# Where GpSimd stops making pauses between indirect DMAs: from the first blocks of the second L1 mixture on

## The chip, the cores and the metric

The kernel runs on one core of a Trainium2 chip. Its time is the device time of one execution, in microseconds (us). A core has these engines: TensorE (PE, with its weight loads shown as PEld), VectorE (DVE), ScalarE (ACT), GpSimd (POOL) and SyncE (SP). Each works through its own queue of instructions in order; semaphores tie them together. Sixteen DMA engines move data between the memories.

## The reference

The input is x, 2048 tokens of 256 features, float32. Two layers follow one another, each made of half a mixture of experts, attention, and half a mixture of experts again:

```python
x = x + 0.5 * moe_L0(layernorm(x))
x = x + attn_L0(layernorm(x))      # a recurrent key-value mix and a channel mix
x = x + 0.5 * moe_L0(layernorm(x))
x = x + 0.5 * moe_L1(layernorm(x))
x = x + attn_L1(layernorm(x))      # linear attention with rotary embedding
x = x + 0.5 * moe_L1(layernorm(x))
```

A mixture scores each token for every expert, takes the best K of them, and adds the weighted outputs of those experts, each of the form `(silu(x @ wg) * (x @ wu)) @ wd`, to that of a shared expert which sees every token. L0 has 8 experts of width 176 and K = 2, L1 has 32 experts of width 96 and K = 6; the shared widths are 352 and 192.

## The kernel before

**Tiles and halves.** The 2048 tokens are 16 tiles of 128. The L1 mixtures and the L1 attention are done in two halves of 8 tiles, A and B, and each half in two groups of 4 tiles. The names of tiles carry the half and the pass: `L_0A` and `L_0B` are the first L1 mixture, `L_1A` and `L_1B` the second, the one that the change is about.

**One mixture of a half** (`sparse_moe`, L402 on) has these steps.
- Routing and plan: scores, the best six, and for each pair of token and expert a slot in a table `xs` in device memory, sorted by expert in blocks of 128 slots. The last step for a group is its index tile (VectorE L576, `idx`).
- `scatter` (L584): GpSimd writes the normalized rows to their slots, by one indirect DMA (L590) for each tile and each of the six choices, so 24 calls a group and 48 a half (`xs_B<-axl_at` is the second mixture's half B).
- Blocks (`step`, L915): for each block of 128 slots SP loads it (`fetch`, L776, after all scatters of the half), PE transposes it (L785, copied by ScalarE at L789), PE multiplies with the expert's gate and up weights (`inner`, L807), ScalarE and VectorE make the gated product (`gates`, L688 and L689), PE turns it (L716, ScalarE L723), PE multiplies with the down weights (`outward`, L825), VectorE evicts the result as `yb` (L833) and SP stores it to `ys` (L835). Five blocks are in work at once, each a step behind the other. 66 blocks are always done; a `tc.If` (L980) holds the rest, for inputs that need more. With these inputs the rest is skipped.
- `gather` (L840): GpSimd fetches the outputs for a tile and a choice back, by an indirect DMA (L847) into one of eight `yk` buffers, again 24 calls a group. The first group's indices (`soon`) need only the first 36 blocks, the second group's (`idx`) need all.
- `add_back` (L858): VectorE adds the weighted rows to x (L859). The buffer is then free for another gather. When a token tile is complete, SP stores it to `out` (L683).
- Shared experts: PE L699, L716, L743 and VectorE L750 add to x. For half B of the second mixture they are spread over the end of its blocks and the time behind them.

**The order of the work** is partly planned while the program is built. `Clock` (L308) holds a planned time, lets a block take 1.41 us of it, a GpSimd call 1.27 (`CALL`) and a pause 1.14 (`PAUSE`), and decides from that between which blocks a call, an addition or a step of the plan is put. `combine` (L890) makes a gather when the planned GpSimd is free, and puts an addition in once more than four gathers are open. `in_turn` (L380) keeps GpSimd's calls in the order planned, `behind_blocks` (L390) puts VectorE's and PE's other work behind the blocks issued so far.

**The pauses.** `called` (L316) counts the GpSimd calls. After each third call `pause` (L326) issues five memsets of a tile `still`, 128 x 96 float32, on GpSimd, one after the other (L331 once, L334 four times); their result is used by nothing. The planner adds 1.14 us for them. A flag decides whether a pause is made:

```python
if len(self.row) == 3:
    if pauses["on"]:
        self.pause()
    else:
        self.row.clear()
        self.still = d.ins
```

The flag is off while the first L0 mixture and the second one send out their tokens (`begin`, L1400), on from there to the last block of the second L1 mixture's half B, and off behind it. Beside the blocks of 1A the 48 scatter calls of 1B are made, then the first group's gathers of 1A; beside those of 1B the second group's gathers of 1A and the first group's of 1B. The second group's gathers of 1B are the tail, after all blocks.

Of the kernel before, what the change touches and what calls it, by code (L numbers as in the profile page):

```python
# [57 lines left out]
def macaron_kernel(ctx: ExitStack, tc: tile.TileContext, a: dict, out: bass.AP):  # L58
# [247 lines left out]
    pauses = {"on": True}  # L306
# [1074 lines left out]
    def all_of(part):  # L1381
        for us in part:
            clock.run(us)
# [6 lines left out]
    def given_rows(m, groups, added, rank=0):  # L1390

        for g in groups:
            yield from wait(lambda: g in m["ready"])
            yield clock.now + 3.0
            yield from m["combine"](g, rank)
            if g == 0 and m["early"] is not None:
                yield from wait(lambda: 0 in m["whole"])
            added.add(g)
# [20 lines left out]
    def settle(*done):  # L1419

        while not all(d() for d in done):
            if fill:
                all_of(fill.pop(0))
            else:
                clock.run(1.0)
# [5 lines left out]
    def pieces_of(part):  # L1431

        return dict(step=lambda: next(part, None), fetch_ahead=lambda: None)

    def filled():
        while fill:
            all_of(fill.pop(0))
# [178 lines left out]
    shared_of(m2[0])  # L1616
    settle(lambda: 1 in sent2[0])
    filled()
    done = [set(), set()]
    clock.begin(4, given_rows(m2[0], range(2), done[0], 4))  # L1620
    all_of(m2[0]["blocks"](lambda: m2[1] if 1 in sent2[1] else None))
# [2 lines left out]
    clock.begin(5, given_rows(m2[1], range(2), done[1], 5))  # L1624
    part = m2[1]["shared"](0, HT)
    all_of(m2[1]["blocks"](lambda: pieces_of(part)))
    pauses["on"] = False
    all_of(part)
    settle(lambda: 1 in done[0], lambda: 1 in done[1])

# [52 lines left out]
```

## Time and profile before

| | |
|---|---|
| median of 6 runs | 1393.07 us (1382.71 to 1395.7) |
| profiled execution, its own time | 1393.51 us |
| its span | 1391.6 us |
| mean granted TensorE clock | 0.916 |
| busy: PE, PEld | 1250.1 us (90%), 950.1 us (68%) |
| busy: DVE, ACT, POOL | 705.5 us (51%), 601.2 us (43%), 653.1 us (47%) |
| scatter calls of 1B, first and last start | 1123.0, 1198.7 us |
| results of 1A's blocks 1, 36 and 66 evicted | 1117.9, 1193.5, 1236.9 us |
| results of 1B's blocks 1 and 66 evicted | 1238.5, 1346.2 us |
| gathers of 1A, first and last start | 1200.0, 1298.0 us |
| gathers of 1B, first and last start | 1303.1, 1382.5 us |

The page of a profile describes one execution. Its times count from the start of the span. A group of instructions is given by line, engine, operation, the tile written and the tiles read, the count, the busy time with the mean of one in ns, and behind a second bar the idle time of the engine just before them with what ended it. A view of waits lists an engine and its instruction, what ended the wait, and then the total, the number of times and the longest. In a table of windows each row is a stretch of the span, with its length and then the busy time and number of instructions of PE, PEld, DVE, ACT and POOL, the granted clock, the mean busy share of the DMA engines and GB/s. In a timeline each row has start and duration in us, and in brackets the idle time before and its releaser. The releaser "remote" stands where none of the core's instructions ends at the time at which the wait does; "issue" stands for time in which nothing that the profile shows was waited for.

### The profile page before, as it was taken

What the parts mean: (1) busy time and instruction counts of PE and PEld (TensorE: products, weight loads), DVE (VectorE), ACT (ScalarE), POOL (GpSimd) and SP (SyncE); (2) the same over time, 40 slices, a digit from 0 to 9 for tenths busy, and PEclk for the clock granted to TensorE, in tenths of its full rate; (3) what the DMA queues carried; (4) which work ended last, traced back from release to release, by engine and by line L of the source; (5) the groups of instructions that cost most, each with busy time, mean ns of one, the idle gap of its engine ahead of it and who ended that gap; (6) DMA issues with size and microseconds to landing.
All of it is one profiled execution on the core that took longest, in us unless ns stands there. A gap on an engine that the chain in (4) does not pass through costs nothing. (4 is left out here: it accounts for less than half of the span.)

```text
span 1391.6 us, 22823 instructions
## 1 busy us (share of the span) xinstructions
PE 1250.1 (90%) x6036; PEld 950.1 (68%) x6036; DVE 705.5 (51%) x2500; ACT 601.2 (43%) x1645; POOL 653.1 (47%) x1267
## 2 busy tenths in 40 slices
PE   7979999899998989999789988989897889989991
PEld 5757776466676757667568865967764677878861
DVE  5422366843424423565354556575576456455653
ACT  4313385775434323444234534544333344444430
POOL 1520344211102510577777557162767457656655
PEclk9879999999998889999969998998899789999995
DMA  9812432992008323433847764643322237778853
GB/s 285 253 65 79 136 117 69 302 324 77 0 0 187 112 87 111 131 114 102 235 142 244 240 206 135 200 132 103 129 85 80 91 124 224 242 216 249 258 155 100
DMA packets 193669, 213.64 MB, mean 154 GB/s; under 512 B 40669, under 2 KB 176509, under 8 KB 193533
## 3 DMA queue, kind: packets, MB, share of 16 engines
q1 hardware_dynamic: 168956, 144.91, 33.9%
q0 software_dynamic: 24576, 67.14, 15.8%
q8 instruction: 59, 0.97, 0.3%
q14 instruction: 78, 0.63, 0.2%
HBM read 101.99 MB, written 109.97 MB: 152 GB/s over the span
## 5 line engine op out<-in xcount | busy, mean ns | idle before, releaser
L847 POOL DMA_INDIRECT yk_L<-ys_L,idx_L x64 | 63.2, 987 | 189.3 <-DMA ys_L<-yb_L 142.8
L334 POOL MEMSET still<- 128x96 f32 x564 | 100.9, 179 | 32.3
L699 PE MATMUL pg_L<-L0sgu,xTs_L 128*128 128x352 f32 x256 | 106.4, 549 | 9.2 <-DVE h_L L689 5.6
L807 PE MATMUL pg_L_b<-L0gu,xbT_L 128*128 x312 | 108.6, 471 | 1.0 <-ACT xbT_L L789 0.6
L590 POOL DMA_INDIRECT xs_L<-xn_L,idx_L x64 | 61.7, 963 | 88.6 <-DVE taken_L L202 29.3
L825 PE MATMUL py_L_b<-L0down,hT_L_b 88*128 x312 | 81.4, 383 | 0.1
L699 PEld LDWEIGHTS pg_L<-L0sgu,xTs_L 128*128 128x128 f32 x256 | 53.1, 224 | 34.5 <-issue 13.7
L689 DVE TENSOR_TENSOR h_L_b<-g_L_b,pg_L_b 128x176 f32<-128x176 f32 x78 | 26.1, 335 | 93.6 <-ACT g_L_b L688 77.4
L825 PEld LDWEIGHTS py_L_b<-L0down,hT_L_b 88*128 88x128 f32 x312 | 59.1, 192 | 19.8 <-issue 1.0
L807 PEld LDWEIGHTS pg_L_b<-L0gu,xbT_L 128*128 128x128 f32 x312 | 55.0, 195 | 20.4 <-issue 1.6
L590 POOL DMA_INDIRECT xs_B<-axl_at,idx_L_1B x48 | 46.3, 965 | 36.9 <-DVE soon_L_1B L578 24.8
L590 POOL DMA_INDIRECT xs_A<-axl_at,idx_L_1A x48 | 46.4, 966 | 35.6 <-DVE soon_L_1A L578 23.6
L807 PE MATMUL pg_L_0B_b<-L1gu,xbT_L_0B 128*128 x264 | 59.1, 350 | 1.4 <-DVEq L980 1.3
L1075 PE MATMUL pkk_cm<-mk_cm,w_WkeyT 128*128 128x512 f32 x128 | 58.7, 594 | 1.4 <-ACT sk_cm L1176 0.9
L807 PE MATMUL pg_L_0A_b<-L1gu,xbT_L_0A 128*128 x264 | 58.8, 348 | 1.1 <-issue 0.8
L807 PE MATMUL pg_L_1B_b<-L1gu,xbT_L_1B 128*128 x264 | 55.7, 335 | 3.9 <-DVE x L859 3.6
L743 PE MATMUL py_L<-L0sdown,hT_L 128*128 128x256 f32 (+1 forms) x192 | 54.3, 421 | 5.1 <-issue 5.0
L1087 PE MATMUL pkv_cm<-w_WvalT,sk_cm 128*128 128x256 f32 x256 | 58.6, 379 | 0.1
L1087 PEld LDWEIGHTS pkv_cm<-w_WvalT,sk_cm 128*128 128x128 f32 x256 | 48.3, 190 | 13.7 <-issue 7.2
L807 PE MATMUL pg_L_1A_b<-L1gu,xbT_L_1A 128*128 x264 | 55.9, 334 | 1.1 <-ACT xbT_L_1A L789 0.4
L688 ACT ACTIVATE g_L<-pg_L 128x176 f32<-128x176 f32 x64 | 19.4, 317 | 84.7 <-PE pg_L L699 45.7
L590 POOL DMA_INDIRECT xs_A<-xn_L_0A,idx_L_0A x48 | 46.5, 969 | 16.1 <-issue 13.1
(667 smaller groups left out, 3296.9 us busy)
## 6 DMA issues: line engine op xcount, KB each, us to landing
xs_A<-zero SPq DMA_DIRECT2D x1, 10112.0 KB
xs_B<-zero SPq DMA_DIRECT2D x1, 10112.0 KB
xb_L<-xs_L SPq DMA_DIRECT2D x78, 128.0 KB
ys_L<-yb_L SPq DMA_DIRECT2D x78, 128.0 KB
xb_L_0A<-xs_A SPq DMA_DIRECT2D x66, 128.0 KB
ys_A<-yb_L_0A SPq DMA_DIRECT2D x66, 128.0 KB
xb_L_0B<-xs_B SPq DMA_DIRECT2D x66, 128.0 KB
ys_B<-yb_L_0B SPq DMA_DIRECT2D x66, 128.0 KB
```

The costliest lines, as they stand in the source:

```text
L334: d = nc.gpsimd.memset(still, 0.0)
L590: d = nc.gpsimd.indirect_dma_start(out=xs, out_offset=bass.IndirectOffsetOnAxis(ap=idx[:, t, k : k + 1], axis=0), in_=sent[g][t - BT * g], ...
L688: nc.scalar.activation(g, pg[:, 0:width], AF.Silu)
L689: nc.vector.tensor_tensor(dst, g, pg[:, width : 2 * width], ALU.mult)
L699: nc.tensor.matmul(pg, xbT[:, c, i * P : (i + 1) * P], w["sgu"][:, c, u, :, :].rearrange("p z w -> p (z w)"), start=(c == 0), stop=(c == D ...
L743: nc.tensor.matmul(py, hT[0:m, k, :], w["sdown"][0:m, k, :], start=(k == 0), stop=(k == len(rows) - 1),)
L807: nc.tensor.matmul(pg, xbT[:, c, :], w["gu"][:, c, bass.ds(e, 1), :, :].rearrange("p e z h -> p (e z h)"), start=(c == 0), stop=(c == DC - 1),
L825: mm = nc.tensor.matmul(py, hT[0:HP, k, :], w["down"][:, bass.ds(e, 1), k, :].rearrange("p e d -> p (e d)"), start=(k == 0), stop=(k == C ...
L847: d = nc.gpsimd.indirect_dma_start(out=yk, out_offset=None, in_=ys[0 : (n + lead) * P, :], in_offset=bass.IndirectOffsetOnAxis(ap=of[:, t, ...
L1075: nc.tensor.matmul(ps, w[:, c, oc * P : (oc + 1) * P], src[:, c, :], start=(c == 0), stop=(c == DC - 1),)
L1087: nc.tensor.matmul(ps, src[:, c, i * P : (i + 1) * P], w[:, c, :], start=(c == 0), stop=(c == n - 1),)
```

## The change

One line moves: the flag goes off before the blocks of 1A, not behind those of 1B. No other line differs.

```diff
     settle(lambda: 1 in sent2[0])
     filled()
+    pauses["on"] = False
     done = [set(), set()]
     clock.begin(4, given_rows(m2[0], range(2), done[0], 4))
     all_of(m2[0]["blocks"](lambda: m2[1] if 1 in sent2[1] else None))
...
     clock.begin(5, given_rows(m2[1], range(2), done[1], 5))
     part = m2[1]["shared"](0, HT)
     all_of(m2[1]["blocks"](lambda: pieces_of(part)))
-    pauses["on"] = False
     all_of(part)
```

In the program as built, the 40 pauses from the second scatter call of 1B on are gone, with their 200 memsets. As the planner counts no 1.14 us for them, it also puts the gathers and the additions (L859) earlier among the blocks: all 24 additions of 1A's first group now come before 1A's `tc.If`, and 1B's first group is added at blocks 42 to 62 instead of 45 and on. ScalarE's order is the same.

## The prediction

> **What bounds the kernel where the change acts.** I read the page's slices first, then the table of windows over the last third, then the waits and the timelines of GpSimd (POOL) and VectorE (DVE). The windows run from the scatter of the second half (xs_B, first call at 1123.0) to the last block of 1B (its result is evicted at 1346.2); the first two columns are the length and PE's busy time:
>
> ```profile
> 1123.00:1200.00 77.00, 71.30 (x420) 60.84 (x419) 40.55 (x156) 34.70 (x124) 60.96 (x129) 0.93 0.62 202
> 1200.00:1237.00 37.00, 36.27 (x226) 32.23 (x225) 19.76 (x61) 19.36 (x75) 20.23 (x42) 1.00 0.80 237
> 1237.00:1242.00 5.00, 2.09 (x12) 1.51 (x11) 3.17 (x9) 1.13 (x4) 2.07 (x7) 0.99 0.68 203
> 1242.00:1300.00 58.00, 55.65 (x328) 49.10 (x328) 32.74 (x99) 26.93 (x108) 39.06 (x81) 0.94 0.81 240
> 1300.00:1345.00 45.00, 44.20 (x254) 37.39 (x253) 26.85 (x82) 20.31 (x82) 30.37 (x64) 1.00 0.76 223
> ```
>
> The reader is to see that PE sets the pace: it is busy for 71.30 + 36.27 + 2.09 + 55.65 + 44.20 = 209.5 of 222 us. All its idle time here is 12.5 us, so no change to GpSimd can win more than that before 1345. GpSimd, the last of the busy columns, is not the bound (152.7 us). Behind 1345 come the 24 last gathers at 1.25 us each (1349.44 to 1382.54 with waits), the last addition and the store; they make no pauses now either.
>
> **What goes.** The order of the instructions on each engine shows what the diff alone would not: 200 memsets vanish from GpSimd, one L331 and four L334 in each of 40 pauses.
>
> ```profile
> L334 POOL MEMSET still<- 128x96 f32 x160 | 28.6, 179 | 9.2
> ...
> L331 POOL MEMSET still<- 128x96 f32 x40 | 7.7, 193 | 0.0
> ```
>
> That is 28.6 + 7.7 = 36.3 us of GpSimd. The 48 scatter calls of xs_B stand in one row, then 24 gathers of 1A, 24 more behind 1A's If, 24 of 1B, 24 more in the tail as now. In the before trace three scatter calls and a pause took 4.8 us (1150.52 to 1155.43, say); three calls alone at 1.265 us take 3.8. So the scatter would need 48 x 1.265 = 61 us in place of 76.7 (1123.01 to 1199.68), if group 1's indices (written at 1155.62) are there in time.
>
> **What the freed time is worth: little.** The blocks came at 40 / 26 = 1.54 us each beside the paused scatter (1160 to 1200) and at 37 / 26 = 1.42 beside the paused gathers (1200 to 1237): if the scatter is over sooner, some 3 us. The first gathers of 1A wait for 36 blocks, and behind those for the additions (POOL yk_L_1A waited 14.2 us in 1200 to 1300 for DVE x L859, since there are eight yk buffers); so an earlier gather is no end by itself. The additions move ahead, one per block: all 24 of 1A's first group stand before the If, where 11 stood behind it, and of 1B's four fewer stand behind the last If. Around 1A's If PE waited 3.6 us for L859: 1.5 to 2 us may go. In the tail four additions, 4 x 0.5 = 2.0 us, no longer stand ahead of the other ones, but GpSimd's 24 calls set the end there, so I take 0.5. Together I take -3 us after overlap, with ends at 0 and at -12.5 - 2 = -14.5.
>
> **What the pauses hide: the dear part.** What do runs of GpSimd calls without a pause do to others? The trace has such runs, all made while pauses were off: 8, 8 and 16 scatter calls of the L0 mixture in 0 to 200 (31.51, 47.11 and 63.12 on), the same three numbers in 445 to 496, and 22 of the tail's gathers (12 from 1353.09, 10 from 1371.16). In just these stretches, the waits have a releaser called "remote": VectorE or ScalarE waits, and what it waits for comes late, from no instruction that ends then. In 0 to 200, 400 to 500 and 1300 to 1392 the lines are (total, times, longest):
>
> ```profile
> ACT g_L L688 <- remote: 12.1, 1, 12.1
> DVE mx_L L178 <- remote: 12.0, 2, 6.4
> ...
> DVE x L750 <- remote: 6.9, 1, 6.9
> ```
>
> ```profile
> ACT L688 <- remote: 7.4, 1, 7.4
> ...
> ACT g_L L688 <- remote: 4.6, 1, 4.6
> ...
> ACT hT_L L723 <- remote: 2.5, 1, 2.5
> ```
>
> ```profile
> DVE x L750 <- remote: 7.7, 2, 4.3
> ```
>
> In 200 to 400 and 500 to 1300, where scatters and gathers of the same kind are paused, there is no such line. Here is one of them, on VectorE in the 16 calls from 63.12 to 83.0:
>
> ```profile
> 72.96 0.22 DVE L674 TENSOR_TENSOR same_L<-same_L,comb_L 128x64 f32<-128x64 f32 x1
> 80.11 0.43 DVE L750 SCALAR_TENSOR_TENSOR x<-py_L,x 128x256 f32<-128x256 f32 x1 [6.92 <-remote]
> ```
>
> L750 adds what PE's L743 wrote; PE's timeline has those matmuls from 70.80 to 72.26. In the paused scatter, VectorE's work on blocks comes in bunches that start in the pauses: its 1.66 us wait for PE ended at 1154.05, and a pause ran from 1154.01 to 1155.27:
>
> ```profile
> 1153.05 0.96 POOL L590 DMA_INDIRECT xs_B<-axl_at,idx_L_1B  x1 [0.30 <-issue]
> 1154.01 0.19 POOL L331 MEMSET still<- 128x96 f32 x1
> 1154.26 1.01 POOL L334 MEMSET still<- 128x96 f32 x4
> 1155.43 0.96 POOL L590 DMA_INDIRECT xs_B<-axl_at,idx_L_1B  x1 [0.16 <-issue]
> ```
>
> My reading: while GpSimd issues indirect DMAs without a break, word of finished matmuls reaches the other engines late; a pause lets it out. The price comes from the lines above, as a share of the calls' time. First 200 us: VectorE lost 12.0 + 6.9 = 18.9 in 32 x 1.26 = 40 us, 47%. 445 to 496: ScalarE lost 7.4 + 4.6 + 2.5 = 14.5 of 40, 36%. Tail: 7.7 of 22 x 1.25 = 27.5, 28%.
>
> The blocks are a chain PE (L807), ScalarE, VectorE, PE (L716), ScalarE, PE (L825), VectorE, three blocks in flight, with PE full: time in which its results go unseen is lost.
> - Scatter, 61 us in one row (or two of 30): 28% to 47% is 17 to 29 us. I take the middle one, 36% or 22 us: both scatter stretches lie at or above it, but the blocks beside the paused calls lose something already, which would be counted twice.
> - Gathers: the first eight of each row find free buffers and run without a break, 3 x 8 x 1.25 = 30 us, at 28% to 47% 8 to 14 us; I take 11. The other 48 need an addition each, and these stand in VectorE's queue behind the blocks' own work: if VectorE is stuck, GpSimd soon waits too, and its wait does a pause's work (in the tail it waited 3.27 us for L859, and L750 went on at 1370.08, before the call at 1371.16). So 0 to 28% of 60 us, 0 to 17 us. I take 3: in the paused stretch such waits were already frequent.
>
> What is queued behind the late instructions: on VectorE the additions and the evictions yb (L833), so the stores, so the gathers, so the tail, which moves as a whole.
>
> **The sum.** 1393.5 (the profiled execution: span 1391.6 and 1.9 around it; 0.4 above the median of 1393.07) + 22 + 11 + 3 - 3 = 1426.5; I forecast **1426**. Ends of this case: 1393.5 + 17 + 8 - 3 = 1415 and 1393.5 + 29 + 14 + 17 = 1453.5.
>
> **A rule against this reading.** The waits on "remote" above are measured. The Trainium skill's page "SBUF — State Buffer", section "Who interferes with whom", states that DMA never contends with a compute engine and that "PE and ACT never wait on anyone"; only VectorE and GpSimd share a port pair. By it, back-to-back calls would delay nothing of PE's, the 36 us terms above would be nothing, and the time would be about 1390. ScalarE's 12.1 us wait on a matmul's result in the unpaused run does not fit it; but a port is not a semaphore's way, on which that section is silent. The trace decides for me.
>
> **Rivals.**
> 1. *Only the first row of scatter calls freezes* (0.15). Group 1's indices (L576) need PE and VectorE; frozen, they come late, GpSimd waits, and the second row starts after the pile has cleared; gathers are held by their additions. Then 24 x 1.265 x 0.28 to 0.47 = 8.5 to 14 us, perhaps +5 more at the gathers, -3: 1399 to 1410, say 1405. For it: the "remote" waits come singly, one or two in a run. Against: the 16-call runs froze most in their second half (80.11, then to 86.05), so length makes it worse.
> 2. *No freeze beside blocks: same or faster* (0.27). The freezes were seen beside shared experts (L699, L743) and routing, not beside routed blocks. If the blocks' results get out in the 0.30 us between calls, the pauses were only 36.3 us of GpSimd's time, and what is left is the gain above: -3 to -14.5, 1379 to 1390.5, likeliest 1389. It decides from the point at which losses fall under 3 us, a tenth of what I count. For it: no unbroken run of this trace lies beside blocks of L1, so their share is carried over, not seen. Against: late and bunched block work beside three calls already, and the 1.54 against 1.42 us per block.
> 3. *More than both* (0.03): denser gathers also meet the block loads (DMA share 0.80 to 0.81 now), over 1453.
>
> That the change does not do what it says is excluded: the 200 memsets are gone from the order.
>
> **How the numbers follow.** Forecast case 0.55, rivals 0.15, 0.27 and 0.03. A measurement tells about 0.5%, 7 us, from no change. Slower: 0.55 + 0.15 + 0.03 = 0.73. Rival 2 splits at 1386: some 0.11 faster, 0.16 within. The range 1386 to 1453 leaves out those 0.11 and the 0.03. The forecast case's own range is 1415 to 1453.
>
> **Signs.** Right, if the changed trace has "remote" waits on ScalarE and VectorE (g L688, hT L723, h L689, yb L833) between 1120 and 1200, PE's busy share there falls to some 70%, and the 36th block of 1A (now evicted at 1193.5) comes some 20 us later although the scatter's calls lie 1.27 us apart. The gathers' share shows as shorter ones in the first 10 us of each row. Wrong, if blocks keep 1.4 to 1.55 us beside unbroken calls; then rival 2 holds. Wrong in size, if the second scatter row shows none (rival 1), or if all 72 gathers show them. The tail behind the last block should stay about 45 us.

## The result, and the profile after

The changed kernel takes **1465.93 us** (median of 20 runs, 1454.88 to 1474.37) where the kernel before takes 1393.71 in 46 runs beside it: 1.0531 times as long, interval 1.0507 to 1.0555. The forecast was 1426 with a range up to 1453. The direction was right, the size less than half of what was measured: 33 us forecast, 72 measured.

The page of the changed kernel begins with its span, and among the groups stands the scatter of 1B:

```profile
span 1464.4 us, 22608 instructions
...
L590 POOL DMA_INDIRECT xs_B<-axl_at,idx_L_1B x48 | 46.4, 967 | 59.7 <-DVE soon_L_1B L578 24.7
```

The busy time of the 48 calls is that of before (46.3 then), but GpSimd sat idle for 59.7 us ahead of them where it was 36.9. GpSimd's timeline shows where: behind the 24th call it waited 21 us for group 1's indices, which had been there in time before (written at 1155.62, with the calls going on).

```profile
1151.34 0.96 POOL L590 DMA_INDIRECT xs_B<-axl_at,idx_L_1B  x1 [0.30 <-issue]
1173.27 0.96 POOL L590 DMA_INDIRECT xs_B<-axl_at,idx_L_1B  x1 [20.97 <-DVE idx_L_1B L576]
```

The table of windows of the changed kernel, cut at GpSimd's rows of calls (first row of scatter calls, the gap, second row, no calls, first gathers of 1A; columns as before: length, then PE, PEld, DVE, ACT, POOL, granted clock, DMA share, GB/s):

```profile
1122.00:1152.30 30.30, 13.31 (x64) 11.12 (x62) 6.94 (x22) 6.93 (x14) 23.11 (x24) 0.66 0.37 126
1152.30:1173.30 21.00, 16.91 (x101) 14.20 (x101) 10.62 (x56) 6.96 (x24) 0.04 (x1) 0.76 0.23 76
1173.30:1203.60 30.30, 14.39 (x57) 9.77 (x55) 7.71 (x26) 3.74 (x15) 23.25 (x24) 0.66 0.42 144
1203.60:1240.00 36.40, 32.80 (x188) 29.61 (x189) 16.13 (x50) 18.15 (x67) 0.00 (x0) 0.86 0.52 158
1240.00:1279.70 39.70, 30.80 (x165) 25.71 (x163) 17.34 (x51) 13.29 (x51) 23.36 (x24) 0.87 0.65 188
```

PE, which was busy for 71.3 of 77 us beside the paused scatter, is busy for 13.3 of 30.3 and 14.4 of 30.3 us beside the two unpaused rows, at a granted clock of 0.66. As soon as GpSimd is silent (fourth row), it is at 32.8 of 36.4 again. The waits in 1100 to 1240 have the "remote" lines that the prediction named as a sign:

```profile
DVE h_L_1A_b L689 <- remote: 20.8, 1, 20.8
...
ACT s_L_1B L190 <- remote: 12.9, 1, 12.9
...
ACT g_L_1A_b L688 <- remote: 9.9, 2, 5.3
...
DVE yb_L_1A L833 <- remote: 7.2, 3, 6.1
```

PE's timeline and VectorE's beside it show the longest of them as it happens:

```profile
1144.92 0.43 PE L716 MATMUL ph_L_1A_b<-ident,h_L_1A_b 128*96 128x128 f32 x1
1156.39 0.45 PE L716 MATMUL ph_L_1A_b<-ident,h_L_1A_b 128*96 128x128 f32 x1 [11.04 <-ACT s_L_1B L190]
```

```profile
1156.09 0.25 DVE L689 TENSOR_TENSOR h_L_1A_b<-g_L_1A_b,pg_L_1A_b 128x96 f32<-128x96 f32 x1 [20.77 <-remote]
```

PE's last matmul ends at 1145.35. Nothing more happens on PE, VectorE or ScalarE until 1156.05, when ScalarE's L190 and VectorE's L689 start together, 3.7 us after GpSimd's last call has ended (1152.30). What the two waited for had been done for 10.7 us.

**Which engine's word is late** can be counted in the trace: for each engine's semaphore, how long after the end of one of its instructions the update comes, counted from the end of the last one before it that makes such an update. In the changed kernel between 1122 and 1280 no update of VectorE or ScalarE that the trace holds comes more than 0.02 us late. PE's come up to 10.7 us late. In the whole trace of before, 211 updates of PE are over 0.15 us late.

**Where the 72.8 us of span came from.** The evictions of 1A's and 1B's blocks cut the time into stretches:

| stretch, us | before | changed | difference |
|---|---|---|---|
| start to 1A's block 1 | 1117.8 | 1117.0 | -0.8 |
| 1A's block 1 to 36 (scatter of 1B) | 75.6 | 117.8 | +42.2 |
| 1A's block 36 to 66 (first gathers of 1A) | 43.5 | 57.7 | +14.2 |
| to 1B's block 1 (1A's If) | 1.6 | 1.2 | -0.4 |
| 1B's block 1 to 36 (second gathers of 1A) | 59.6 | 68.1 | +8.5 |
| 1B's block 36 to 66 (first gathers of 1B) | 48.1 | 58.3 | +10.2 |
| tail | 45.4 | 44.2 | -1.2 |

### The profile page after: what moved, and what is told of

The parts are those of the page before. It is cut to its first block, busy times and chain, and to the rows that moved or that the text cites. A ratio compares the mean times of both kernels' runs of the same rounds, so it can differ in the third digit from the quotient of the medians.

```text
span 1464.4 us, 22608 instructions
## 1 busy us (share of the span) xinstructions
PE 1268.0 (87%) x6036; PEld 962.6 (66%) x6036; DVE 706.5 (48%) x2500; ACT 605.3 (41%) x1645; POOL 618.0 (42%) x1067
## 5 line engine op out<-in xcount | busy, mean ns | idle before, releaser
L334 POOL MEMSET still<- 128x96 f32 x404 | 72.4, 179 | 23.3
L590 POOL DMA_INDIRECT xs_B<-axl_at,idx_L_1B x48 | 46.4, 967 | 59.7 <-DVE soon_L_1B L578 24.7
L689 DVE TENSOR_TENSOR h_L_b<-g_L_b,pg_L_b 128x176 f32<-128x176 f32 x78 | 26.2, 336 | 93.4 <-ACT g_L_b L688 78.2
L807 PE MATMUL pg_L_1A_b<-L1gu,xbT_L_1A 128*128 x264 | 60.3, 354 | 3.1 <-issue 2.5
L807 PE MATMUL pg_L_1B_b<-L1gu,xbT_L_1B 128*128 x264 | 59.3, 350 | 3.7 <-issue 2.6
L689 DVE TENSOR_TENSOR h_L_1A_b<-g_L_1A_b,pg_L_1A_b 128x96 f32<-128x96 f32 x66 | 16.6, 252 | 80.4 <-ACT g_L_1A_b L688 47.0
L825 PE MATMUL py_L_1A_b<-L1down,hT_L_1A_b 96*128 x132 | 45.1, 426 | 11.1 <-issue 5.9
```

The lines of the kernel that those rows point to most:

```text
L334: d = nc.gpsimd.memset(still, 0.0)
L590: d = nc.gpsimd.indirect_dma_start(out=xs, out_offset=bass.IndirectOffsetOnAxis(ap=idx[:, t, k : k + 1], axis=0), in_=sent[g][t - BT * g], ...
L689: nc.vector.tensor_tensor(dst, g, pg[:, width : 2 * width], ALU.mult)
L807: nc.tensor.matmul(pg, xbT[:, c, :], w["gu"][:, c, bass.ds(e, 1), :, :].rearrange("p e z h -> p (e z h)"), start=(c == 0), stop=(c == DC - 1),
L825: mm = nc.tensor.matmul(py, hT[0:HP, k, :], w["down"][:, bass.ds(e, 1), k, :].rearrange("p e d -> p (e d)"), start=(k == 0), stop=(k == C ...
```

## The experiments

Theory: rows of GpSimd's DMA calls without a break hold back PE's semaphore updates; a pause lets them out; the loss is that and nothing else. Rival: the planner's new order (additions earlier in VectorE's queue) costs the time. A second rival came up on the way: that the late updates only go with the loss. Of each change to the kernel the main lines are shown; dots stand for the others, which mostly set a switch.

### One part alone

*scatter_alone*: the kernel before, with the flag off while 1B's scatter is made.

```diff
-            sent[h].add(g)
+            sent[h].add(g) or (h, g) == (1, 1) and pauses.update(on=True)
...
-    done = [set(), set()]
+    done, pauses["on"] = [set(), set()], False
```

> The pauses are left out of the 46 scatter calls of 1B alone (from the third call on) and made again at the gathers. Theory (runs of GpSimd DMA calls without a break hold back PE's semaphore updates, and a pause lets them out): the loss of the changed kernel up to 1A's 36th block, 42 us, returns nearly whole, and beside the gathers the pace is that of before: 1393.7 + 42 = 1436, between 1428 and 1442. Rival (the order of the additions costs the time): under 1405.

*gathers_alone*: the other half of the change, off from the end of that scatter on.

```diff
-            sent[h].add(g)
+            sent[h].add(g) or (h, g) == (1, 1) and pauses.update(on=False)
```

> The pauses are left out from the end of 1B's scatter on, so at 72 gathers and at no scatter call. Theory: the changed kernel lost 14.4 us from 1A's block 36 to 66, 8.4 to 1B's block 36 and 10.3 to its block 66, together 33: 1393.7 + 33 - 1 = 1426, between 1415 and 1432; the two parts add up to the whole. Rival (the late scatter spoils the gathers' stretch, so the gathers alone cost little): under 1405.

In both kernels the planner counts other pauses than in the kernel before, so each has an order of the additions of its own. In gathers_alone 1A's begin at block 53, as in the kernel before (the changed kernel has 41), but come about one per block; 1B's stand as in the changed kernel.

*order_alone*: the planner as in the changed kernel, the memsets issued.

```diff
-                if pauses["on"]:
+                if pauses["on"] or pauses.get("free"):
...
-            self.pool += PAUSE
+            self.pool += PAUSE if pauses["on"] else 0.0
...
-    pauses["on"] = False
+    pauses.update(on=False, free=True)
...
```

> The order of the changed kernel on every engine, with the 40 pauses issued all the same; only the planner does not count them. Theory: the memsets are what helps, so the time is near that of before, 1390 to 1405, the excess from additions that stand in VectorE's queue ahead of their gather. Rival (the earlier additions in VectorE's queue are what costs): 1440 or more.

*memsets_alone*: the planner as before, the memsets from 1A's blocks on not issued.

```diff
-                if pauses["on"]:
+                if pauses["on"] and not pauses.get("silent"):
...
-                    self.still = d.ins
+                    self.still, self.pool = d.ins, self.pool + PAUSE * pauses["on"]
...
```

> The planner counts the 40 pauses and orders all other work as in the kernel before, but the 200 memsets are not issued. Theory: as slow as the changed kernel, 1450 to 1475. Rival (the order costs the time): 1390 to 1405.

The kernel before took 1389.86 us beside these four:

| kernel | median, us | ratio | 1A 1 to 36 | 36 to 66 | 1B 1 to 36 | 36 to 66 |
|---|---|---|---|---|---|---|
| scatter_alone | 1440.11 | 1.0358 (1.0325 to 1.0391) | 117.9 | 45.6 | 60.4 | 48.4 |
| gathers_alone | 1426.90 | 1.0262 (1.0235 to 1.0289) | 73.9 | 57.6 | 68.6 | 58.2 |
| order_alone | 1414.41 | 1.0165 (1.0128 to 1.0201) | 73.6 | 57.4 | 61.6 | 53.2 |
| memsets_alone | 1449.89 | 1.0431 (1.0398 to 1.0464) | 117.8 | 50.0 | 65.5 | 53.3 |

In the scatter's stretch the missing memsets explain all: 117.8 or 117.9 us in the three kernels without them, 73.6 and 73.9 with them. Order does nothing there. Each part alone has the changed kernel's figures in its own stretch. By the medians the two parts add up to more than the whole, 50 + 37 against 72. From 1A's block 1 to 1B's block 66 they nearly agree with it: 45.2 + 32.2 = 77.4 us against 74.7. Much of the excess lies ahead of 1A's first block, which in these four traces comes 1 to 6 us later than in that of before, where the kernels do not yet differ.

The two parts came out as expected. memsets_alone lies just under its range (1449.89 against 1450 to 1475), and order_alone, expected at 1405 at most, missed: it took 1414.41.

At the gathers the theory alone is too simple. With the old order and no memsets (memsets_alone) the three stretches lose 6.5 + 5.9 + 5.2 = 17.6 us, in the changed kernel 32.9, in gathers_alone 14.1 + 9.0 + 10.1 = 33.2. And the new order with the memsets (order_alone) loses 21 us there. The waits of these kernels from 1200 to 1420 say something of it. In order_alone:

```profile
DVE x L859 <- DMA yk_L_1A<-ys_A,soon_L_1A: 22.5, 20, 3.9
```

In memsets_alone, and then in gathers_alone:

```profile
POOL yk_L_1A L847 <- DVE x L859: 28.1, 7, 17.8
```

```profile
POOL yk_L_1A L847 <- DVE x L859: 34.6, 7, 16.4
```

With paused calls and the new order, additions stand in VectorE's queue ahead of data that is not there, and the blocks' work queues behind them. Late updates are not what costs the time there: from 1A's block 36 to 1B's block 66, those of PE that are over 0.15 us late add up to 17 us in order_alone and to 22 in before.

With unpaused calls GpSimd runs ahead and then waits for additions. The length of these waits does not tell the kernels apart, since gathers_alone waits as long as memsets_alone and loses nearly twice as much. What differs is how close the gathers come. In memsets_alone the 72 gathers come in 24 rows (a new row begins behind over 0.6 us of idle time), three calls each on average, and PE's late updates add up to 46 us. In the changed kernel it is 19 rows and 64 us, in gathers_alone 17 rows and 75 us. In both of these the additions come about one per block, in memsets_alone they are more widely spaced.

So the rival holds for a part: about 60 us of the 72 are the missing memsets in the old order, and the other 12 come with the new order. That they come because the gathers run in closer rows is a reading that these counts support; no run sets the length of a row by itself.

### What must a pause be, and what holds the updates back?

Four kernels asked this. From 1A's blocks on, a pause is one memset; or one tensor_tensor of 128 x 256; or five memsets after each sixth call; or the changed kernel has calls of half the bytes.

```diff
-            for _ in range(4):
+            for _ in range(0 if pauses.get("short") else 4):
...
```

> From 1A's blocks on a pause is one memset in place of five, so GpSimd's gap between two calls is about 0.5 us in place of 1.3 after each third call (0.30 without a pause); the order of all other work is that of before. If the pause helps by the time in which no call is issued: most of the loss of the kernel without memsets (60 us) comes back, 1425 to 1450. If any instruction that is no DMA call, however short, lets PE's updates out: 1388 to 1400.

```diff
-                d = nc.gpsimd.memset(still, 0.0)
+                d = nc.gpsimd.tensor_tensor(*[pauses["long"]] * 3, ALU.add) if pauses.get("short") else nc.gpsimd.memset(still, 0.0)
...
```

> A pause is one tensor_tensor of 128 x 256 (0.8 us where the kernel uses the same kind) in place of five memsets, so one instruction and a gap of about 1.1 us. If the length of the gap counts: near before, 1385 to 1402. If it is the spaces between the five short instructions, or memsets as such, that let the updates out: over 1420.

```diff
-                if pauses["on"]:
+                if pauses["on"] and not (pauses.get("short") and pauses.update(odd=not pauses.get("odd")) is None and pauses["odd"]):
...
```

> Every second pause is left out, so five memsets after each sixth call, in the order of before. Theory: PE's updates are held up once some three to eight calls stand in a row, so a part of the 60 us comes back: 1405 to 1435. If a row of six is still harmless: 1385 to 1398.

```diff
-                            out=xs,
+                            out=xs if pauses["on"] else xs.rearrange("n (h d) -> (n h) d", h=2),
...
-                            in_=sent[g][t - BT * g],
+                            in_=sent[g][t - BT * g] if pauses["on"] else sent[g][t - BT * g][:, 0:128],
...
```

The gathers and the additions are halved in the same way.

> The changed kernel with the same calls and the same number of rows in each, but 128 columns of each row in place of 256 (half the bytes); what is scattered and gathered is therefore not what the mixture needs, and the additions are half as wide. If it is the bytes on the DMA engines that hold back PE's updates: at least half of the 72 us goes, 1405 to 1435. If it is GpSimd's issuing of the calls: the freezes beside the scatter stay, and the time is over 1450.

| kernel | median, us | before beside it | ratio |
|---|---|---|---|
| one_memset | 1352.11 | 1351.56 | 0.9994 (0.9955 to 1.0033) |
| one_sum | 1347.55 | 1351.56 | 0.9957 (0.9923 to 0.9991) |
| every_sixth | 1356.25 | 1351.56 | 1.0011 (0.9976 to 1.0045) |
| half_rows | 1349.56 | 1351.56 | 0.9969 (0.9939 to 0.9998) |

All four are within 0.5% of the kernel before, even the one without any pause, and the kernel before itself is 40 us faster than in all runs until then. This was another chip. In these four traces not one wait has "remote" as its releaser, and not one of PE's updates is over 0.15 us late, but for two at the program's end. The runs tell nothing of pauses, but they allow a test of the cause: the changed kernel itself, run again, with three of these beside it.

> The changed kernel itself, as a control beside the three others. In the last call the kernel before took 1351.56 us in place of 1389.86, and in the traces of that call no update of PE's semaphore was late. Theory (the loss is PE's late updates and nothing else): where before takes about 1390, this is 65 to 80 us slower and PE's updates are late; where before takes about 1350, updates are punctual and this is within 10 us of before. Rival (the loss has another cause, and the late updates only go with it): slower by over 20 us in both cases.

It took 1352.01 us, the kernel before 1354.37: 0.9991 (0.9954 to 1.0028). The windows of this run over the two rows of 1B's scatter:

```profile
1093.70:1124.00 30.30, 27.43 (x157) 23.78 (x156) 15.79 (x72) 13.38 (x36) 23.20 (x24) 0.83 0.49 167
1124.00:1155.40 31.40, 31.40 (x199) 27.86 (x198) 20.41 (x72) 17.93 (x67) 23.26 (x24) 1.00 0.85 274
```

Calls as dense as in the first run of the changed kernel (24 in 30.3 us), and PE is busy for 27.4 and 31.4 us in place of 13.3 and 14.4; the second row starts 1.2 us behind the first, not 21. So the same program loses 72 us or nothing, and what differs in the traces is whether PE's updates are late. The second rival had the loss in both cases, and that is ruled out: where no update is late, there is no loss. Of the six chips that the record numbers, three showed late updates, with before at 1390 to 1393 us, and three did not, with before at 1351 to 1354. Why chips differ in this, no run tells.

One more thing goes with the late updates. The trace of before holds 4842 updates of the semaphores of PE, VectorE, ScalarE and GpSimd for 6485 instructions that make one; that of after_again holds 6265 for 6285. All eight traces with late updates lack 21 to 26% of them, and some of each of the four engines; the twelve others lack under 1%. So the counts of late updates above are counts of those that a trace holds, and whether the two have one cause stays open. The waits themselves do not rest on these counts: PE, VectorE and ScalarE stand still in the timelines above.

The three beside it (one_memset_2 1349.79 us, every_sixth_2 1350.57, half_rows_2 1348.46, each with a ratio between 0.995 and 1.000 to before) and two later ones (one_memset_3 1.0015, half_rows_3 0.9948 with an interval of 0.9921 to 0.9975) came on chips of the second sort as well, and so did the last run, with a ratio of 1.0001:

> As every_sixth: from 1A's blocks on five memsets after each sixth call, in the order of before. Where updates are late: 10 to 40 us slower than before, as rows of eight calls lost four to six of ten us in the trace of before; within 7 us if rows of six are harmless. Where before takes about 1350: the same.

Half the bytes win some 0.5% there. To get several answers from one run, I put them into separate stretches of one kernel (group 0 and 1 of 1A's scatter, then of 1B's).

> The kernel before with pauses in both L0 scatters; in the scatter of 1A one memset as a pause (group 0) and five after each sixth call (group 1); in that of 1B half of each row and no pause (group 0; half of each row is left out in both its groups), and one tensor_tensor as a pause (group 1). Where updates are late (before at about 1390): none are late in the L0 scatters; PE's busy share beside half rows without a pause is about 45%, as in the changed kernel, if the calls count, and over 70% if the bytes do; beside one memset and every sixth call some are late, by 1 to 4 us; beside one sum none is late by over 1.2 us. Where they are not (before at about 1350): within 10 us of before.

```diff
-    HT = NT // 2
+    HT, MODES = NT // 2, {(0, 0): "one", (0, 1): "six", (1, 0): "none", (1, 1): "sum"}
...
-            yield from m[h]["scatter"](g, rank)
+            yield from (pauses.update(mode=MODES[h, g], half=h == 1), m[h]["scatter"](g, rank))[1]
...
-        pauses["on"] = False
+        pauses["on"] = True
...
```

It came on a chip with late updates (before 1393.35 us, mix 1431.51). Its windows over the scatter rows with one memset, with half rows and no pause, and with one tensor_tensor:

```profile
962.90:993.50 30.60, 11.70 (x55) 8.91 (x55) 6.98 (x25) 5.15 (x14) 24.54 (x31) 0.67 0.37 129
1134.00:1164.10 30.10, 13.12 (x63) 10.92 (x61) 6.85 (x22) 6.89 (x14) 23.01 (x24) 0.66 0.25 80
1185.20:1219.60 34.40, 25.92 (x120) 18.83 (x118) 14.48 (x46) 9.74 (x37) 28.27 (x32) 0.89 0.44 141
```

The places of the first and the third row in the trace of before, with five memsets after each third call:

```profile
975.70:1001.00 25.30, 21.36 (x106) 17.97 (x107) 12.08 (x55) 11.21 (x28) 20.15 (x42) 0.80 0.39 132
...
1161.00:1199.70 38.70, 37.17 (x227) 32.17 (x226) 19.24 (x62) 18.20 (x76) 30.68 (x65) 1.00 0.77 247
```

- Half the bytes (second row; 80 GB/s in place of 126): PE is busy for 13.1 of 30.1 us, with full rows it was 13.3 of 30.3. **The calls hold the updates back, not their bytes.** Each call still writes as many rows, so whether it is the issuing or the number of rows stays open.
- One memset (first row): PE is busy for 11.7 of 30.6 us (21.4 of 25.3 with five memsets in the same place of before), updates are up to 12.1 us late. A pause of one short instruction is none.
- One tensor_tensor (third row; its rows are half ones too): 25.9 of 34.4 us (75%), updates up to 1.9 us late. It lies between no pause at all (14.4 of 30.3 us, 47%, in the second row of the changed kernel) and the five memsets (37.2 of 38.7 us, 96%, in the same place of before).

The share of PE beside half rows was expected at about 45% if the calls count, and was 44%. The lateness was not forecast well: up to 4 us was expected beside one memset, at most 1.2 beside one tensor_tensor.

GpSimd's timeline shows what these leave between two calls, first the one memset, then the tensor_tensor:

```profile
965.47 0.96 POOL L590 DMA_INDIRECT xs_A<-axl_at,idx_L_1A  x1 [0.30 <-issue]
966.42 0.20 POOL L331 MEMSET still<- 128x96 f32 x1
966.79 0.97 POOL L590 DMA_INDIRECT xs_A<-axl_at,idx_L_1A  x1 [0.17 <-issue]
```

```profile
1186.45 0.96 POOL L590 DMA_INDIRECT xs_B<-axl_at,idx_L_1B  x1 [0.31 <-issue]
1187.44 0.62 POOL L331 TENSOR_TENSOR long_one<-long_one 128x256 f32<-128x256 f32 x1
1188.23 0.99 POOL L590 DMA_INDIRECT xs_B<-axl_at,idx_L_1B  x1 [0.16 <-issue]
```

The gap is 0.36 us with one memset, hardly over the 0.30 without any, 0.82 us with the tensor_tensor, and 1.42 us with the five memsets of before (1154.01 to 1155.43), beside which the updates were at most 1.05 us late. So PE's share grows with the time without a call. One instruction does little or much by its length, so their number is not what counts; but these are three lengths, each in another stretch, and what lies between 0.82 and 1.42 was not tried. Every sixth call was tried in mix too (no update late in 28 us), but beside work that differs from the blocks, so that it stays open how long a row may be.

### A faster version

In mix the two L0 scatters had pauses as well, and the first scatter of the first L1 mixture began at 574.0 in place of 592.7. Late updates in the two L0 stretches fell from 20 and 17, the latest by 4.5 us, to 4 and 4, the latest by 0.8. Alone this is one word of the kernel before:

```diff
     def begin(m, ahead):
...
-        pauses["on"] = False
+        pauses["on"] = True
```

> The kernel before with pauses also in the two L0 scatters (64 calls, some 20 pauses of 1.1 us), where its trace has 31 and 21 us of late updates. Where before takes about 1390: the late updates there go; 10 to 25 us faster if these lie on the path, within 5 if the shared experts beside them have slack. Where before takes about 1350: 0 to 20 us slower, by the pauses themselves.

> As pauses_at_L0: the kernel before with pauses also in the two L0 scatters. In mix these brought the first call of 1A's predecessor (xs_A of the first L1 mixture) from 592.7 to 574.0, so where updates are late I expect before minus 12 to 22 us, about 1375; if the earlier start is lost again further on, within 5 us of before. Where before takes about 1350: no difference.

Where no update is late it made no difference, 1.0012 (0.9976 to 1.0048). Where they are late it took **1377.86 us against 1392.18: 0.9883 (0.984 to 0.9927)**, faster than both kernels, and near the 1375 that was expected. In its trace the late updates of the two L0 stretches are 5 and 5, the latest by 0.8 us, and the first scatter of the first L1 mixture begins at 584.3. Its 20 or so pauses of about 1.1 us are more than paid by the updates that they let out, and where none is late the unchanged time says that they lie beside work that lasts longer.

## Why the prediction was wrong

The mechanism was forecast and is shown: rows of calls without a pause hold back word of PE's work. The terms for its size failed.

- **Gain, "-3 us after overlap".** About right, as far as it can be seen. The If gave 0.4 in place of 1.5 to 2, the tail 1.2 in place of 0.5. On a chip without late updates, where nothing else acts, the whole change is worth 0.9991 (0.9954 to 1.0028), so at most some 6 us: there rival 2 holds, at its lower gain.
- **Scatter, "I take the middle one, 36% or 22 us".** This is the step that failed: 42.2 us measured, 69% of the 61 us of calls, over the upper end of 29. I had priced the loss by the "remote" lines of one engine; in 445 to 496 VectorE had waited for "remote" too, 4.7 us at L545 and 2.0 at L178. The share did not carry over from one sort of work to another. In one of the L0 stretches that I priced it by (63.1 to 86.0 of before) PE, which had shared experts to work on, was busy for 15.5 of 22.9 us; beside the blocks it was busy for 13.3 of 30.3. My reading, which no run isolates: a block hands over from PE to another engine four times, so each late update stops the next step. The routing and plan of 1B is one more such chain, and the trace shows it pushed behind the first row: hence the gap of 21 us, in which blocks come at 3.0 us each (7 in 21 us) in place of 1.5. The "remote" lines of one engine show too little of this even here: VectorE's largest two in 1100 to 1240 add up to 20.8 + 7.2 = 28 us of the 42.
- **"Group 1's indices ... if they are there in time."** They were not, by 21 us; rival 1 had seen this, but took it for a relief. After 1156.1 no update in the gap was late, and then the second row froze as much as the first (14.4 of 30.3 us busy).
- **Gathers, "the other 48 need an addition each ... I take 3".** Wrong by its reason. This is the second step that failed. I took over the waits for L859 from the paused trace, though the change itself moves the additions forward, one per block; the first gathers of 1A then went in one row of 11 calls (1240.12 to 1252.94). 14.2 + 8.5 + 10.2 = 33 us against 11 + 3, just over the upper ends of the two terms, 14 + 17. memsets_alone, where the additions stay where they were, loses 17.6, near the 14 forecast: the argument held for the order of before, and the change removes that order.
- **"For it: the 'remote' waits come singly"** (rival 1): not so beside blocks.
- **A rule against this reading.** By the Trainium skill's page "SBUF — State Buffer", section "Who interferes with whom", a DMA never contends with a compute engine. The prediction worked out from it a time without these losses. The changed kernel's 1352.01 us beside 1354.37 agrees with that, its 1465.93 beside 1393.71 does not. What is late there is word of PE's work, on which that section is silent. The measurement decides, and it differs by chip.
- **The range** left out what no trace of before could have shown, that the size depends on the chip; but the measured time lies on the side where the range's end, 1453, was the sum of ends that were each too low.

## What to carry to other kernels

When a profile's waits end on a releaser that is no instruction, look at which engine's semaphore updates come late and at what another engine does without a break in just that time; a loss priced beside one sort of work can be too low for other work (here 22 us were forecast and 42 measured), above all where a chain that is held up stands in the way of the next row of calls. A pause that looks like idle work may be what lets others go on: before it is taken out, see what the trace shows in stretches that lack it, and put it where it is missing. And a cost that is seen on one chip is measured on another before it is put down to the kind of chip.

## What was not expected of the hardware

- The same program (the kernel before) takes 1390 to 1394 us on some chips and 1351 to 1354 on others; in the traces the difference goes with PE's semaphore updates, which are late (211 by over 0.15 us in the trace of before) or never late. The reason is not known.
- The updates of PE alone are late, those of VectorE and ScalarE are not (0.02 us at most beside the rows of calls), as far as the traces hold them.
- Twenty-four indirect calls of 1.27 us in a row hold back PE's updates up to 10.7 us with 256 columns in each row of data, up to 9.3 us with 128. With 0.82 us without a call after each third, PE is busy for 75% of the time where it is 96% with 1.42 us; with 0.36 us for 38% where it is 84%.
